# Four graph layers, stage of adj: layer 0's table rows stored from ACT's queue, and other ranks for the stage's pieces

## The chip, the cores and the metric

The kernel runs on one core of a Trainium2 chip. A core has five engines with a queue of instructions each: PE (matrix products), DVE (vector), ACT (scalar), POOL (general) and SP, which only starts transfers. Instructions of one queue go in order; queues wait for one another through semaphores. Transfers are moved by 16 DMA engines that all queues share. The metric is the device time of one execution in microseconds (us); lower is better.

## The reference, cut to what matters

3327 nodes with 512 float32 features each pass through four residual layers. All four use the same adjacency matrix, 3327 x 3327 int32, in which an entry is 1 with a probability of 0.0012, some four neighbours a node.

```python
def reference(x, adj, ...):
    # layer 0: mean over neighbours
    h = relu(layernorm(x))
    mask = adj > 0
    agg = mask @ h / max(deg, 1)
    x = x + relu(concat(h @ W_self + b_self, agg @ W_nb + b_nb) @ W_comb + b_comb)
    # layer 1: attention, 8 heads of 64; layer 2: 4 heads, quaternion weights, elu; layer 3: 1 head
    for attend in (layer1, layer2, layer3):
        h = relu(layernorm(x))
        Wh = h @ W                      # [n, heads, o]
        e = leaky_relu(src(Wh)[:, None] + dst(Wh)[None, :])
        x = x + act(softmax(where(adj > 0, e, -inf)) @ Wh)
    return x
```

No layer needs the dense product with adj: a node's sum runs over its few neighbours. The kernel finds them once and gathers rows. In layer 0 the two products behind each other are folded: `wf[1]` = W_nb · W_comb (lower half), `wf[0]` = W_self · W_comb (upper half), so a node needs z = h · `wf[1]` of its neighbours and y = h · `wf[0]` of itself.

## The kernel before, in words

The nodes lie in 26 tiles of 128 rows (the last has 127). A first stage, the stage of adj, does everything up to the first gather; then four layers run, in which POOL gathers rows of a table in device memory, PE sums them and makes the next table. Only the first stage is touched.

**Reading adj.** Each tile of adj is loaded in two halves of 128 x 1664 (`ai`, 832 KB, four buffers; line 1184, on SP). DVE finds the places of the ones in each half (line 1209, two instructions); ACT squares it with a running sum (line 1217, `junk`), which counts the ones for a check at the end. A buffer comes free when both have read it. From the places DVE makes lists of neighbours and degrees, and POOL writes them as a record beside the node's row (lines 1261 to 1267).

**Layer 0's rows.** Tiles go in pairs, in the order `SEQUENCE` (0 to 19, 25, 20 to 24). For each: x is loaded (SP, line 1184 too), DVE takes mean and variance (1309), ACT and DVE make the norm from it, ACT writes h (1328), PE transposes it into `pt` (1337), ACT copies that to `hT` (1342), and PE makes two products of four row blocks: z in `pz` and y in `py` (both line 1349). On the page a product of one tile counts as eight matmuls. ACT copies z to `zt` (two buffers; line 1358, or 1361 for the short tile) and the copy is stored, 256 KB, as the tile's rows of `table[0]` (line 1366). ACT copies y into the node's own row (1373).

**Weights.** Before any z, PE transposes W_nb and makes the four blocks of `wf[1]` (line 976; line 953 transposes), and the same with W_self for `wf[0]`; the blocks are copied by ACT and DVE in turn (line 989 ACT, 987 DVE). Later come the bias, the transposes of the last layer's weight W3 (PE 1094, copy on ACT 1100) and the products of weights with the attention vectors (POOL 1131), which DVE (1148), or ACT for the last layer (1142), sums.

**The sort.** When all tiles are searched, DVE makes a table of degree classes (1394), PE sums it (`pm_tot`, 1406), DVE works out each node's place (1419 to 1427), and POOL scatters the nodes' own rows (x, y and record) to their places in `own` (1435), one instruction per tile. SP reads the records back (1451), DVE makes degrees of them (1505, 1506), and the first gather of layer 0 starts (1562).

**What sets the order.** The instructions' order on each queue is worked out ahead of time by the class `Plan`. It keeps a list of pieces, each with an engine, an estimated cost, a rank, what it depends on, and the buffers that it takes and gives. It then plays the stage through: always the piece that can start earliest is taken, and among those that can start at the same time the one of lowest rank. Pieces on `"dma"` are transfers in this play and issue nothing. The helper `load` puts an issue on SP, cost 0.38, and a transfer behind it. The ranks come from eight numbers: `ORDER_W` gives those of the weights (1 and 0 for the two folded weights, the bias, and "later" for the other layers' weights); the adj tile at position k has `ADJ`·k; the pair that begins at position p0 has `WORK`·p0 + `WORK0`; its loads of x have `X0` + `X`·p0; y comes `SELF` later in rank than z. The sort has -1. The scatters, the read back and the degrees come behind the plan, in that order.

Of the kernel before, what the change touches and what calls it, by code (L numbers as in the profile page):

```python
# [8 lines left out]
F32 = mybir.dt.float32  # L9
# [9 lines left out]
P = 128  # L19
# [673 lines left out]
def gnn_stack_kernel(  # L693
# [19 lines left out]
    nc = tc.nc  # L713
    N, D = x_in.shape
# [20 lines left out]
    with ExitStack() as st:  # L735
# [82 lines left out]
        def rough(pool, tag, var, scale=1.0):  # L818

            n = var.shape[-1]  # L820
            ln = pool.tile([P, 2], F32, tag="ln", name=f"ln{tag}", bufs=3)[:, :n]
            nc.scalar.activation(ln, var, AF.Ln, bias=eps, scale=scale)
            r0 = pool.tile([P, 2], F32, tag="r0", name=f"r0{tag}", bufs=3)[:, :n]
            nc.scalar.activation(r0, ln, AF.Exp, bias=lift, scale=-0.5)
            return r0

        def refined(pool, tag, mv, r0):

            n = r0.shape[-1]
            a = pool.tile([P, 2], F32, tag="nra", name=f"nra{tag}", bufs=3)[:, :n]  # L830
            nc.vector.scalar_tensor_tensor(a, r0, -1.0, r0, ALU.mult, ALU.mult)
            nc.vector.scalar_tensor_tensor(a, mv[:, :, 1], EPS, a, ALU.add, ALU.mult)
            r = pool.tile([P, 2], F32, tag="rs", name=f"rs{tag}", bufs=3)[:, :n]
            nc.vector.scalar_tensor_tensor(r, a, 3.0 * LIFT * LIFT, r0, ALU.add, ALU.mult)
            nmr = pool.tile([P, 2], F32, tag="nmr", name=f"nmr{tag}", bufs=3)[:, :n]
            nc.vector.scalar_tensor_tensor(nmr, mv[:, :, 0], -1.0, r, ALU.mult, ALU.mult)
            return r, nmr

        def refined_sums(pool, tag, mv, r0):

            n = r0.shape[-1]
            a = pool.tile([P, 2], F32, tag="nra", name=f"nra{tag}", bufs=3)[:, :n]
            nc.vector.scalar_tensor_tensor(a, r0, -1.0 / D, r0, ALU.mult, ALU.mult)
            nc.vector.scalar_tensor_tensor(a, mv[:, :, 1], D * EPS, a, ALU.add, ALU.mult)
            r = pool.tile([P, 2], F32, tag="rs", name=f"rs{tag}", bufs=3)[:, :n]
            nc.vector.scalar_tensor_tensor(r, a, 3.0 * LIFT * LIFT, r0, ALU.add, ALU.mult)
            nmr = pool.tile([P, 2], F32, tag="nmr", name=f"nmr{tag}", bufs=3)[:, :n]
            nc.vector.tensor_tensor(nmr, mv[:, :, 0], r, ALU.mult)
            return r, nmr


        with tc.tile_pool(name="p0", bufs=1) as pa, tc.tile_pool(name="p0p", bufs=2, space=PSUM) as pp:
# [5 lines left out]
            later = pa.tile([P, NK - EARLY, ROW], F32, tag="later", name="later")  # L858
# [31 lines left out]
            bias = part("bias", D)  # L890
# [20 lines left out]
            plan = Plan(limits)  # L911
            tiles = {}
# [257 lines left out]
            o = put("pool", 3.0, (0.5, 0), empty_rows)  # L1170
# [125 lines left out]
            rows_in = []  # L1296
            for p0 in range(0, NK, 2):
                unit = SEQUENCE[p0 : p0 + 2]
                rank = (p0 * WORK + WORK0, 2)
                box = {}  # L1300
                seen = []
                for j, i in enumerate(unit):
                    o = load((X0 + p0 * X, j), 4.0 * P * D, start_x, (i,), free_at(i))

                    def stats(j=j, i=i, unit=unit, box=box):
                        if j == 0:
                            box["mv"] = new("mv", f"n{unit[0]}", [P, 2, 2])
                        st6 = pa.tile([P, 6], F32, tag="st6", name=f"st6n{i}", bufs=2)
                        nc.vector.bn_stats(st6, node(i)[:, :D])
                        nc.vector.bn_aggr(box["mv"][:, j, :], st6)  # L1310

                    seen.append(put("dve", 0.88, rank, stats, (), [o] + seen, take=("mv",) if j == 0 else ()))

                def guess(unit=unit, box=box):
                    box["r0"] = rough(pa, f"n{unit[0]}", box["mv"][:, :, 1])

                o = put("act", 0.6, rank, guess, (), seen)

                def refine(unit=unit, box=box):
                    box["r"], box["nmr"] = refined(pa, f"n{unit[0]}", box["mv"], box["r0"])  # L1320

                normed = put("dve", 0.8, rank, refine, (), [o], take=("norm",), give=("mv",))
                for j, i in enumerate(unit):
                    key = f"n{i}"

                    def relu(j=j, i=i, key=key, box=box):
                        h = new("h", key, [P, D])
                        nc.scalar.activation(
                            h, node(i)[:, :D], AF.Relu, bias=box["nmr"][:, j : j + 1], scale=box["r"][:, j : j + 1]
                        )  # L1330

                    o = put("act", 0.83, rank, relu, (), [normed], take=("h",), give=("norm",) if j == 1 else ())

                    def turn(key=key):
                        pt = new("pt", key, [P, DC, P], space=pp)
                        for c in range(DC):
                            nc.tensor.transpose(pt[:, c, :], tiles["h", key][:, c * P : (c + 1) * P], ident)

                    o = put("pe", 0.55, rank, turn, (), [o], take=("pt",), give=("h",))

                    def keep(key=key):
                        nc.scalar.copy(new("hT", key, [P, DC, P]), tiles["pt", key])  # L1342

                    o = put("act", 0.6, rank, keep, (), [o], take=("hT",), give=("pt",))

                    def multiply(s, tag, key=key):
                        pz = new(tag, key, [P, D], space=pp)
                        for c in range(DC):
                            nc.tensor.matmul(  # L1349
                                pz, tiles["hT", key][:, c, :], wf[s][:, c, :], start=(c == 0), stop=(c == DC - 1)  # L1350
                            )

                    z = put("pe", 3.5, rank, multiply, (1, "pz"), [o] + finished[1], take=("pz",))

                    def keep_z(i=i, key=key):
                        zt = new("zt", key, [P, D])
                        if i < NK - 1:
                            nc.scalar.copy(zt, tiles["pz", key])
                        else:

                            nc.scalar.activation(zt, tiles["pz", key], AF.Copy, scale=real[:, i : i + 1])

                    o2 = put("act", 0.62, rank, keep_z, (), [z], take=("zt",), give=("pz",))

                    def store(i=i, key=key):
                        nc.sync.dma_start(table[0][i * P : (i + 1) * P, :D], tiles["zt", key])
# [20 lines left out]
            o = put("dve", 0.3, sorting, work, (), [f for k in range(NK) for f in found_of[k]], take=("ai",))  # L1387
# [44 lines left out]
            landed = []  # L1432
# [83 lines left out]
        with tc.tile_pool(name="run", bufs=1, reuse_waits="tile") as pr, tc.tile_pool(  # L1516
# [9 lines left out]
            plan = Plan(limits)  # L1526
# [733 lines left out]
```

## Time and profile before

| what | value |
|---|---|
| median of three runs | 1074.55 us (1073.38 to 1076.67) |
| the profiled execution | 1231.77 us |
| its span in the records | 1230.0 us |
| granted PE clock, mean | 0.855 |
| first stage, to the first gather | 0 to 278.18 us |
| PE / DVE / ACT busy, whole span | 73% / 59% / 42% |

All positions below are us from the start of the span of the one profiled execution. That execution was 15% longer than the median of the runs without a profile, so differences are taken from its own times. A line of waits says which instruction waited, what it waited for, how long in total, how often, and the longest. A line of the timeline gives start and length of an instruction or a row of like ones, and in brackets the idle time of its engine ahead of it and what ended it. "SPq" is SP's queue, whose instructions only start transfers.

Two figures stand behind several of the prediction's steps. A product of one tile takes PE 3.44 us (24 matmuls in a row, three products, take 10.46 us at 214.65, the last one's end included). The 22 scatters from 219.24 to 246.36 follow each other at 1.26 us.

### The profile page before, as it was taken

The numbers are of one execution on the slowest core, as the hardware profiler recorded it, in microseconds if no ns is written. First come the engines' busy times: TensorE is split into PE (matmuls) and PEld (weight loads), VectorE is DVE, ScalarE is ACT, GpSimd is POOL, SyncE is SP. The second block draws the span as 40 slices with busy tenths as digits, with TensorE's granted clock in tenths as the row PEclk, the third lists the DMA queues.
The fourth block names the chain that finished last, engine by engine and source line by source line (L and its number), as shares of the span: only waits on it lengthen the run. The fifth ranks groups of instructions, "written<-read, shape, count | busy, mean of one in ns | idle before, by whom it ended". The sixth has DMA issues, their size and how long they took to land. (4 is left out here: it accounts for less than half of the span.)

```text
span 1230.0 us, 11605 instructions
## 1 busy us (share of the span) xinstructions
PE 901.8 (73%) x2853; PEld 510.4 (41%) x2853; DVE 726.6 (59%) x1848; ACT 518.2 (42%) x1700; POOL 610.1 (50%) x719
## 2 busy tenths in 40 slices
PE   7599999854098889752979796539979832948865
PEld 4244444322075656531647464214435421423322
DVE  6499989204176557453869784628894815534441
ACT  4488886210043433422656553316554621312221
POOL 1064246717655550175757511766883236675661
PEclk9899999977599899966989889659896956978987
DMA  9999894958587772265666521665754345575561
GB/s 352 338 364 338 294 306 146 317 203 286 172 268 252 247 249 89 76 195 149 198 183 178 154 79 55 189 187 150 209 169 129 91 121 149 168 206 160 163 186 59
DMA packets 89910, 240.49 MB, mean 196 GB/s; under 512 B 24933, under 2 KB 26477, under 8 KB 89834
## 3 DMA queue, kind: packets, MB, share of 16 engines
q0 software_dynamic: 41600, 137.72, 38.1%
q1 hardware_dynamic: 48234, 101.96, 23.3%
q8 instruction: 24, 0.39, 0.1%
q14 instruction: 52, 0.43, 0.1%
HBM read 190.35 MB, written 49.27 MB: 195 GB/s over the span
## 5 line engine op out<-in xcount | busy, mean ns | idle before, releaser
L1562 POOL DMA_INDIRECT ring<-table,nbr x351 | 368.5, 1050 | 185.5 <-issue 80.9
L1593 PE MATMUL acc<-ring,ident 128*128 128x512 f32 (+1 forms) x494 | 266.6, 676 | 66.8 <-DVE ring L2110 24.3
L1780 PE MATMUL pw<-w,hT 128*128 128x264 f32 (+1 forms) x832 | 197.3, 394 | 18.3 <-ACT hT L1705 13.6
L1780 PEld LDWEIGHTS pw<-w,hT 128*128 128x128 f32 x832 | 161.2, 195 | 60.9 <-ACT hT L1705 20.5
L1593 PEld LDWEIGHTS acc<-ring,ident 128*128 128x128 f32 (+1 forms) x494 | 98.7, 215 | 175.1 <-issue 107.5
L1562 POOL DMA_INDIRECT ring<-table,srec x117 | 110.1, 941 | 77.8 <-issue 31.5
L2110 DVE TENSOR_TENSOR ring<-ring,w 128x2048 f32<-128x2048 f32 (+7 forms) x76 | 114.3, 1531 | 4.7 <-DVE w L1978 3.0
L2060 PE MATMUL pw<-w,hT 128*128 128x512 f32 x208 | 101.7, 634 | 13.3 <-ACT hT L2052 11.0
L1209 DVE FIND_INDEX8 fidx<-one_i,ai 128x8 uint32<-128x832 int32 x104 | 104.2, 1018 | 0.0
L1349 PE MATMUL pz_n<-wf,hT_n 128*128 128x512 f32 x208 | 95.2, 609 | 10.9 <-ACT hT_n L1342 8.4
L1705 ACT ACTIVATE hT<-pt 128x128 f32<-128x128 f32 (+1 forms) x312 | 81.8, 292 | 39.7 <-PE pt L1694 18.5
L1217 ACT ACTIVATE junk<-ai 128x1664 int8<-128x1664 int32 (+1 forms) x52 | 82.7, 1590 | 32.6 <-DMA ai<-in_adj_dram 32.2
L1694 PE MATMUL pt<-ident,h 128*128 128x128 f32 x208 | 36.5, 312 | 75.9 <-ACT h L1676 73.4
L1349 PE MATMUL py_n<-wf,hT_n 128*128 128x512 f32 x208 | 91.9, 592 | 0.0
L1803 ACT COPY t<-pw 128x512 f32<-128x512 f32 (+1 forms) x54 | 30.6, 566 | 134.0 <-PE pw L1780 43.9
L1941 DVE TENSOR_TENSOR e<-ring,fs 128x24 f32<-128x24 f32 (+25 forms) x96 | 15.2, 172 | 120.2 <-DMA ring<-table,nbr 102.0
L2060 PEld LDWEIGHTS pw<-w,hT 128*128 128x128 f32 x208 | 42.3, 207 | 73.2 <-issue 51.3
L1705 ACT ACTIVATION_READ_ACCUMULATOR hT<-pt 128x1 f32 x312 | 69.5, 223 | 0.0
L1694 PEld LDWEIGHTS pt<-ident,h 128*128 128x128 f32 x208 | 28.1, 160 | 96.3 <-ACT h L1676 81.6
L2194 POOL MEMSET mark<- 1x1 f32 x3 | 0.3, 88 | 132.7 <-DMA table<-t 132.7
L1349 PEld LDWEIGHTS pz_n<-wf,hT_n 128*128 128x128 f32 x208 | 39.8, 195 | 62.8 <-issue 49.4
L2046 PE MATMUL pt<-ident,y 128*128 128x128 f32 x96 | 16.4, 312 | 67.4 <-issue 56.8
(185 smaller groups left out, 1319.7 us busy)
## 6 DMA issues: line engine op xcount, KB each, us to landing
ai<-in_adj_dram SPq DMA_DIRECT2D x25, 832.0 KB
ai<-in_adj_dram SPq DMA_DIRECT2D x25, 831.5 KB
table<-t SPq DMA_DIRECT2D x52, 258.0 KB
xy<-own SPq DMA_DIRECT2D x26, 512.0 KB
table<-t SPq DMA_DIRECT2D x26, 260.0 KB
table<-zt_n SPq DMA_DIRECT2D x26, 256.0 KB
ring<-table,nbr POOLq DMA_INDIRECT x351
later<-in_x_dram SPq DMA_DIRECT2D x15, 256.0 KB
```

Of the source, the lines that this page charges most:

```text
L1209: nc.vector.max_index(fidx[:, i, qq * 8 : (qq + 1) * 8], one_i, ai[:, q * QW : min(cols, (q + 1) * QW)])
L1217: nc.scalar.activation(junk[:, :cols], tiles["ai", key][:, :cols], AF.Square, accum_out=sq[:, i, hf : hf + 1])
L1349: nc.tensor.matmul(pz, tiles["hT", key][:, c, :], wf[s][:, c, :], start=(c == 0), stop=(c == DC - 1))
L1562: nc.gpsimd.indirect_dma_start(out=ring[:m, r0 + s, : width[layer]], out_offset=None, in_=table[layer], in_offset=bass.IndirectOffsetOnAxi ...
L1593: nc.tensor.matmul(acc, ident[:m, :], g[:m, s, :D], start=(k == 0), stop=(k == len(slots) - 1))
L1694: nc.tensor.transpose(pt[:, c, :], h[:, c * P : (c + 1) * P], ident)
L1705: nc.scalar.activation(hT[:, c, :n], pt[:, c, :n], AF.Copy, accum_out=hsum[layer][:, i, c : c + 1])
L1780: nc.tensor.matmul(pw[:, b, :w], tiles["hT", key][:, c, :], wsb[layer][:, c, b, :w], start=(c == 0), stop=(c == DC - 1),)
L1803: nc.scalar.copy(t[:, :D].rearrange("p (b f) -> p b f", b=2)[:, lo:hi, :], pw[:, lo:hi, :HD])
L2046: nc.tensor.transpose(pt[:, c, :], tiles["y", key][:, c * P : (c + 1) * P], ident)
L2060: nc.tensor.matmul(pw[:, 0, :], tiles["hT", key][:, c, :], w3[:, c, :], start=False, stop=(c == DC - 1))
L2110: nc.vector.tensor_tensor(v, v, box["w"][:m, j, lo:hi, :].unsqueeze(3).to_broadcast([m, hi - lo, H, O]), ALU.mult,)
```

## The change

There are three edits. The store of `zt` is started by ACT (`nc.scalar`) instead of SP, and in the plan it is a piece on ACT of cost 0.35 with a transfer behind it. The eight numbers behind the ranks get other values. The plan's transfer of a scatter costs 1.5 instead of 2.0. Besides, four small tiles of the norm become three columns wide, of which as many are used as before.

```diff
-ORDER_W = {1: -20.0, 0: -1.0, "bias": -4.0, "later": 20.0}
-ADJ, WORK, WORK0, X0, X, SELF = 1.0, 1.13, 1.2, -14.0, 1.77, 7.0
+ORDER_W = {1: -37.41, 0: -0.2, "bias": -17.46, "later": 14.56}
+ADJ, WORK, WORK0, X0, X, SELF = 1.0, 1.18, 0.3, -20.32, 2.18, 4.08
...
-            ln = pool.tile([P, 2], F32, tag="ln", name=f"ln{tag}", bufs=3)[:, :n]
+            ln = pool.tile([P, 3], F32, tag="ln", name=f"ln{tag}", bufs=3)[:, :n]
...
                     def store(i=i, key=key):
-                        nc.sync.dma_start(table[0][i * P : (i + 1) * P, :D], tiles["zt", key])
-
-                    rows_in.append(load(rank, 4.0 * P * D, store, (), [o2], give=("zt",)))
+                        nc.scalar.dma_start(table[0][i * P : (i + 1) * P, :D], tiles["zt", key])
+
+
+                    o2 = put("act", 0.35, rank, store, (), [o2])
+                    rows_in.append(plan.add("dma", 4.0 * P * D / 370e3, rank, None, [o2], lag=2.0, give=("zt",)))
...
-                landed.append(plan.add("dma", 2.0, (-1.0, pos), None, [o], lag=1.5))
+                landed.append(plan.add("dma", 1.5, (-1.0, pos), None, [o], lag=1.5))
```

What comes out as the order on each queue: the four blocks of `wf[0]` and the bias stand ahead of the first z on PE; the load of W3 (1 MB) stands ahead of adj tile 2 on SP; ACT's copy of the first `wf[0]` block stands ahead of its count of that tile instead of behind it, and DVE's copy of the second block behind that tile's finds. W3's transposes are spread between products, and the sums of line 1142 come earlier on ACT, as do POOL's products of line 1131. `pm_tot` stands on PE ahead of z of tile 20 instead of behind it. The loads of x of the last tiles stand ahead of the last adj loads on SP. The 26 stores follow their `zt` copies on ACT. Behind the stage the order on DVE's and SP's queues is the same as before.

More of the change, by code (lines that the diff above doesn't have):

```diff
@@ L820, in rough @@
             n = var.shape[-1]
-            ln = pool.tile([P, 2], F32, tag="ln", name=f"ln{tag}", bufs=3)[:, :n]
+            ln = pool.tile([P, 3], F32, tag="ln", name=f"ln{tag}", bufs=3)[:, :n]
             nc.scalar.activation(ln, var, AF.Ln, bias=eps, scale=scale)
-            r0 = pool.tile([P, 2], F32, tag="r0", name=f"r0{tag}", bufs=3)[:, :n]
+            r0 = pool.tile([P, 3], F32, tag="r0", name=f"r0{tag}", bufs=3)[:, :n]
             nc.scalar.activation(r0, ln, AF.Exp, bias=lift, scale=-0.5)
@@ L829, in refined @@
             n = r0.shape[-1]
-            a = pool.tile([P, 2], F32, tag="nra", name=f"nra{tag}", bufs=3)[:, :n]
+            a = pool.tile([P, 3], F32, tag="nra", name=f"nra{tag}", bufs=3)[:, :n]
             nc.vector.scalar_tensor_tensor(a, r0, -1.0, r0, ALU.mult, ALU.mult)
             nc.vector.scalar_tensor_tensor(a, mv[:, :, 1], EPS, a, ALU.add, ALU.mult)
-            r = pool.tile([P, 2], F32, tag="rs", name=f"rs{tag}", bufs=3)[:, :n]
+            r = pool.tile([P, 3], F32, tag="rs", name=f"rs{tag}", bufs=3)[:, :n]
             nc.vector.scalar_tensor_tensor(r, a, 3.0 * LIFT * LIFT, r0, ALU.add, ALU.mult)
-            nmr = pool.tile([P, 2], F32, tag="nmr", name=f"nmr{tag}", bufs=3)[:, :n]
+            nmr = pool.tile([P, 3], F32, tag="nmr", name=f"nmr{tag}", bufs=3)[:, :n]
             nc.vector.scalar_tensor_tensor(nmr, mv[:, :, 0], -1.0, r, ALU.mult, ALU.mult)
@@ L841, in refined_sums @@
             n = r0.shape[-1]
-            a = pool.tile([P, 2], F32, tag="nra", name=f"nra{tag}", bufs=3)[:, :n]
+            a = pool.tile([P, 3], F32, tag="nra", name=f"nra{tag}", bufs=3)[:, :n]
             nc.vector.scalar_tensor_tensor(a, r0, -1.0 / D, r0, ALU.mult, ALU.mult)
             nc.vector.scalar_tensor_tensor(a, mv[:, :, 1], D * EPS, a, ALU.add, ALU.mult)
-            r = pool.tile([P, 2], F32, tag="rs", name=f"rs{tag}", bufs=3)[:, :n]
+            r = pool.tile([P, 3], F32, tag="rs", name=f"rs{tag}", bufs=3)[:, :n]
             nc.vector.scalar_tensor_tensor(r, a, 3.0 * LIFT * LIFT, r0, ALU.add, ALU.mult)
-            nmr = pool.tile([P, 2], F32, tag="nmr", name=f"nmr{tag}", bufs=3)[:, :n]
+            nmr = pool.tile([P, 3], F32, tag="nmr", name=f"nmr{tag}", bufs=3)[:, :n]
             nc.vector.tensor_tensor(nmr, mv[:, :, 0], r, ALU.mult)
```

## The prediction

> **What bounds the kernel now.** The edits lie in the first stage: reading adj, sorting the nodes by degree, making layer 0's rows. I read first the busy time of each engine in stretches of it (columns: stretch, its length, busy us and instructions of PE, PEld, DVE, ACT and POOL, granted clock, DMA share, GB/s).
>
> ```profile
> 50.00:100.00 50.00, 47.15 (x126) 21.73 (x126) 47.35 (x120) 42.91 (x63) 19.33 (x35) 0.98 0.97 384
> 100.00:150.00 50.00, 50.00 (x142) 23.82 (x141) 47.10 (x145) 43.79 (x65) 16.49 (x56) 1.00 0.85 302
> 150.00:200.00 50.00, 47.62 (x139) 22.40 (x138) 43.18 (x118) 37.20 (x60) 25.90 (x48) 1.00 0.81 275
> 214.00:250.00 36.00, 26.83 (x74) 12.32 (x73) 9.22 (x32) 8.51 (x17) 25.43 (x39) 0.95 0.94 324
> ```
>
> From 50 to 200 us PE works 144.8 of 150 us, DVE 137.6, ACT 123.9: nothing has much slack, ACT most. After 214 everything has slack except the transfers. Next, what PE waits for up to 280 us (line waited for, total us, times, longest):
>
> ```profile
> PE pm_w L976 <- ACT wf L989: 10.3, 1, 10.3
> PE pz_n L1349 <- ACT hT_n L1342: 8.4, 2, 7.7
> PE pm_w L1094 <- ACT w L1100: 1.6, 1, 1.6
> PE pm_tot L1406 <- DVE ai_sort L1394: 1.3, 1, 1.3
> ```
>
> The 10.3 us lie at 38 to 49, the 7.7 at 244 to 251, so between 60 and 214 PE loses only about 3. Then SP's queue, up to 215 us:
>
> ```profile
> SPq L1184 <- DVE fidx L1209: 58.7, 29, 4.9
> SPq L1366 <- ACT zt_n L1358: 34.5, 12, 9.8
> SPq L1366 <- ACT zt_n L1361: 10.2, 1, 10.2
> ```
>
> Line 1366 is the store that moves. For 44.7 us SP stood before one of them until ACT had made its tile, with adj loads queued behind; the larger wait, 58.7, is DVE freeing adj buffers. Last, the timelines of PE and of ACT where the stage ends (start, length, instruction, idle before it):
>
> ```profile
> 214.30 0.34 PE L1406 MATMUL pm_tot<-ai_sort,ones 128*128 128x416 bf16 x1 [1.25 <-DVE ai_sort L1394]
> 251.33 6.20 PE L1349 MATMUL pz_n<-wf,hT_n 128*128 128x512 f32 x8 [7.70 <-ACT hT_n L1342]
> 257.38 10.46 PE L1349 MATMUL py_n<-wf,hT_n 128*128 128x512 f32 x24
> ```
> ```profile
> 239.29 0.58 ACT L1342 COPY hT_n<-pt_n 128x512 f32<-128x512 f32 x1 [5.08 <-issue]
> 250.69 0.58 ACT L1342 COPY hT_n<-pt_n 128x512 f32<-128x512 f32 x1 [10.82 <-remote]
> ```
>
> The sort starts at 214.30 with pm_tot; POOL's scatters of the nodes' own rows run from 219.24 without a break, the 22nd at 246.36, 1.26 us apart, and the DMA share is 0.94 meanwhile. ACT's two waits fall in that burst, have no producer named, and the second ends 3.4 us after the last scatter's issue finished (247.3). Then PE does four products (z of tile 24, y of 22, 23, 24) up to 267.84, the last scatter goes at 269.21, and 10.3 us after PE's end the first gather of layer 0 starts, at 278.18.
>
> **What the skill says.** The Trainium skill, "DMA: Bandwidth & Descriptors", section Issuing engines are not separate DMA queues: transfers run on the same 16 DMA engines whoever starts them, and only the sequencer's time is divided. So the moved store brings no bandwidth; it frees SP from its place in the queue. The trace of before can't test this, ACT starts no transfer in it. "Perfetto Trace Analysis", section DMA Instruction — HWDGE: the issuing sequencer is busy until the descriptors are handed over, and the movement is not in that time. The trace agrees: an issue of line 1366 takes 0.327 us (median of 26, longest 0.751) for 256 KB.
>
> **The change, part by part.**
>
> *Store on ACT.* 26 issues leave SP and enter ACT, each directly behind its zt copy. Price on ACT: 0.33 us, SP's row, plus the drain of the copy ahead; both bounds are open, since before has none. Low end 0.33, high end about 1.5 if the issue keeps ACT for the copy's drain and a slot in the queue; I take 0.55. ACT is idle 29.6 of the 154 us from 60 to 214 (124.42 busy), and 22 stores fall there: 12.1 us at 0.55. The cover is that idle time, 1.35 us a store; above it ACT becomes the bound. Queued behind a store on ACT are the next hT copy, h and the counting of adj, so PE would feel it first through hT. Nine of the 26 also wait for an older transfer's semaphore; those were mostly long done in before. I put the direct cost at 0.
>
> *SP without them.* 8.5 us of issues go (26 x 0.327) and the 44.7 us of waiting. But most adj loads were held by DVE's finds anyway, and DVE was short of adj data only 20.1 us from 46 to 219, of which 12.8 is one wait near 46. The other 7.3 can shrink; I take two thirds, 4.9 us. DVE's sort input, done at 214.25, comes at about 209.4. The x loads of the last tiles, at 212.93 in before behind a store that waited 10.2 us, now precede the last adj loads.
>
> *New order, start.* PE now makes all four wf0 blocks and the bias ahead of the first z; ACT's copy of block 0 stands ahead of the count of adj tile 2 instead of behind it, so the 10.3 us wait shrinks. But W3's 1 MB load now precedes adj tile 2 on SP (the trace lands 832 KB in 2.1 to 2.7 us: about 2.5 us later), and the copy of block 1 on DVE stands behind that tile's find. By hand: fourth block at 54.3 instead of 56.68, second z done at 64.8 instead of 64.0. Cost 0.8 us.
>
> *New order, middle.* W3's transposes and their copies are spread out: PE's waits of 1.6 at 156.45 and 0.7 at 161.23 go, gain 2.3. The attention sums on ACT (line 1142) move from 204 to 213 into 166 to 181, where h of tiles 18 and 19 would be ready at 186.9 and PE needs them at 187.7: 0.8 of slack.
>
> *New order, the sort.* pm_tot stands on PE before z of tile 20 instead of behind it: one product (3.44 us) moves behind the sort. PE could reach pm_tot at 214.30 - 1.25 + 0.8 - 2.3 - 3.44 = 208.1; DVE is ready at 209.4, which decides. So sort and scatters start 4.9 us earlier, scatters at about 214.3, burst over at 241.5. POOL's records (212.88 to 218.94 in before) must be earlier too; they can, since eight products of line 1131 that POOL did from 203 to 212.9 are done earlier.
>
> *The tail.* Behind pm_tot PE has 12 products and four sets of transposes, about 43 us (before 11, 39.6). If PE were held by its work alone, the end would move by 4.9 - 3.44 = 1.5 earlier. But in before it was held by ACT, until the burst ended; I take the hold to end with the burst. Then z of 24 starts at 246.4, and the same four products and 10.3 us follow. The small tiles' third column, and the scatter's price in the plan, issue nothing: 0. SP's read back of the sorted records is no longer queued behind two stores, but waited for the scatters anyway: 0.
>
> Sum: -4.9, all of it the burst; the early +0.8 and the middle -2.3 are hidden by DVE ahead of the sort. The profiled execution took 1231.77 us (span 1230.0), 15% over the median of 1074.55; the stage alone would have to be separated from that excess, which no view does, so I carry the difference unscaled: 1231.8 to 1226.9 profiled, 1074.55 - 4.9 = 1069.65, say 1069.7.
>
> **The rivals.** About 3.2 us (0.3%) is what a measurement tells from no change.
>
> *ACT becomes the bound* (slower). For: ACT is at 81% from 60 to 214, each store stands ahead of an hT copy, and tiles 18 and 19 have 0.8 us of slack. It decides above 1.35 us a store on average; at 1.55 it would cost 22 x 0.2 = 4.4 us, at 2 us 14.3. A local form: a block of sums at 166 to 181 delays hT by some 6 us which PE never gets back. Time 1078 to 1089, middle 1080. Against: SP's 0.33 us.
>
> *Hidden or given back* (same). DVE's work, not adj data, sets the sort: its idle time doesn't shrink, pm_tot stays near 213, the added product behind it eats the rest. For: DVE is busy 142.5 of 154 us. Time 1073 to 1076.
>
> *The whole tail wait goes* (larger gain). ACT's 5.08 and 10.82 us have no producer; if ACT, with its order changed, escapes them, PE's 2.2 and 7.7 us go, and the clock which made one product 6.20 instead of 3.6 recovers: 9.9 + 2.6, less part of the 3.44. With DVE's gain 1058 to 1063. Against: the cause, a full DMA, remains.
>
> *The store doesn't free SP*: adj loads wait for semaphores that ACT's stores now raise, so SP still stops behind them. It ends as the hidden case.
>
> **How the numbers follow.** Likeliest case 0.51 (1067 to 1072.5, of which 0.42 is faster by the bound and 0.09 same), the whole tail 0.11 (faster), hidden 0.10 (0.08 same, 0.02 slower), ACT bound 0.28 (0.27 slower, 0.01 same). Faster 0.53, same 0.18, slower 0.29. Range 1060 to 1081: it leaves out half of the whole-tail case and about a third of the ACT case, some 0.15 in all.
>
> **What would show it.** Right: the scatters start near 214 and pm_tot waits for DVE by a microsecond or two; SP has no wait of zt; PE's wait for wf is a few us; ACT's store issues are 0.3 to 0.6 us; the first gather starts near 273. Wrong: hT waits of PE between 60 and 210 (ACT bound); pm_tot near 213; ACT's nameless waits ending far from the last scatter, or none; loads of adj later than before at 46 by more than 3 us.

## The result: a third of a per cent slower

The changed kernel takes 1079.35 us (median of 18 runs) against 1075.47 for the kernel before, a ratio of 1.0038 with a 95% interval of 1.0021 to 1.0054. The forecast was 1069.7; the sign was wrong, and the measured time lies inside the range.

At some times every run, of whatever kernel here, takes about 1220 us instead of 1074, and the profiled execution that the prediction used was one of these. A second profile of the kernel before, of an execution of 1073 us, is therefore the one to compare with; it is called the second profile of before here. The two differ mainly behind the stage (952 us against 805 from the first gather to the end) and in the tail: ACT's two waits of 5.08 and 10.82 us, on which the forecast's tail was built, aren't in the second, and PE, which had slack behind the sort in the first, has none (35.71 of 36 us busy):

```profile
214.00:250.00 36.00, 35.71 (x96) 16.65 (x95) 7.92 (x29) 9.95 (x19) 26.08 (x36) 1.00 0.94 323
```

In the second profile of before PE waits for this, up to the last product of the stage:

```profile
PE pm_w L976 <- ACT wf L989: 10.7, 1, 10.7
PE pm_w L953 <- DMA later<-in_L_gnn_W_nb_dram: 6.4, 1, 6.4
PE pm_w L976 <- DVE wf L987: 2.7, 1, 2.7
```

In the changed kernel (lines from 1366 on are two higher, so pm_tot is line 1408):

```profile
PE pm_w L976 <- DVE wf L987: 17.4, 1, 17.4
PE pm_w L953 <- DMA later<-in_L_gnn_W_nb_dram: 6.4, 1, 6.4
PE pt_n L1337 <- ACT h_n L1328: 6.0, 1, 6.0
```

With the small ones, left out here, these are 22.2 and 31.0 us, 8.8 more. The last product of the stage ends at 253.5 in before and at 262.7 in the changed kernel, 9.2 later, with as many products in both. So the order of the work, not its amount, moved PE's end. The two places are seen on PE's timeline of the changed kernel:

```profile
56.15 5.97 PE L976 MATMUL pm_w<-later 128*128 128x512 f32 x8 [17.38 <-DVE wf L987]
...
183.61 1.11 PE L1337 MATMUL pt_n<-ident,h_n 128*128 128x128 f32 x4 [5.97 <-ACT h_n L1328]
184.52 4.86 PE L1349 MATMUL py_n<-wf,hT_n 128*128 128x512 f32 x8
...
219.22 0.34 PE L1408 MATMUL pm_tot<-ai_sort,ones 128*128 128x416 bf16 x1
```

and the same place in the second profile of before:

```profile
212.88 0.34 PE L1406 MATMUL pm_tot<-ai_sort,ones 128*128 128x416 bf16 x1 [0.80 <-DVE ai_sort L1394]
```

Both stalls cost more than their length. The Trainium skill, "TensorE: Matmul & The Clock Gate", section Part 1: The HAM clock gate, says that PE falls to half its clock after an idle window of a few microseconds and needs as long to come back. The trace agrees in kind: the granted clock is 0.50 from 56 to 60 and from 184 to 186, and 1.00 from 62 and from 188 on; the eight matmuls behind the 17.38 us gap take 5.97 us, those behind the 5.97 us gap 4.86, others 3.60. Before pays some of this too: its block behind the 10.7 us gap takes 5.32.

The sort comes 6.3 us late (219.22 against 212.88), the first scatter 5.8 (223.66 against 217.83), the first gather of layer 0 6.3 (272.75 against 266.49). From there to the end the two profiles take 803.7 and 804.5 us, so the loss lies in the stage. Its size is better taken from the medians: they differ by 3.9 us, not 6.3, and a profile is one execution. The windows of before, then of the changed kernel (columns as in the prediction), show where engines fell idle:

```profile
50.00:100.00 50.00, 47.34 (x127) 21.98 (x126) 46.05 (x117) 41.54 (x60) 19.34 (x35) 0.98 0.97 379
...
150.00:200.00 50.00, 48.81 (x142) 22.95 (x141) 44.05 (x121) 37.28 (x61) 25.66 (x48) 1.00 0.80 276
```
```profile
50.00:100.00 50.00, 43.85 (x114) 20.50 (x115) 46.52 (x118) 40.77 (x58) 26.16 (x67) 0.89 0.94 362
...
150.00:200.00 50.00, 44.03 (x118) 20.51 (x116) 41.69 (x122) 33.27 (x61) 27.11 (x48) 0.93 0.73 244
```

From 50 to 100 PE loses 3.5 us of work, from 150 to 200 4.8; in the second stretch DVE (2.4), ACT (4.0) and the transfers lose too. All of them wait for each other there.

PE isn't the only engine that comes late to the sort. DVE's table of degree classes is ready at 217.8 against 212.8, 5.0 later, and PE adds 1.5 behind it. Of DVE's waits from 40 to 218, first in before, then in the changed kernel, the one for adj is as long as it was; those for POOL's products and for the norm's first part on ACT have grown:

```profile
DVE fidx L1209 <- DMA ai<-in_adj_dram: 19.1, 5, 13.3
...
DVE nran L831 <- ACT r0n L824: 1.2, 1, 1.2
```
```profile
DVE fidx L1209 <- DMA ai<-in_adj_dram: 18.9, 5, 16.6
DVE w L1148 <- POOL later L1131: 5.1, 2, 2.8
DVE nran L831 <- ACT r0n L824: 5.0, 2, 4.3
```

The longest of each of these two, 2.8 and 4.3 us, end at 168 and 178.5, in the same stretch as PE's second stall.

How that stall comes about can be followed in the changed kernel. POOL's records of tiles 12 to 17 wait for DVE's lists, and stand ahead of the clearing of tile 25's two adj buffers (line 1200):

```profile
158.16 0.63 POOL L1261 TENSOR_SCALAR none<-nid,null_f 128x96 f32<-128x96 f32 x1 [2.97 <-DVE nid L1255]
...
163.86 2.91 POOL L1200 MEMSET ai<- 128x1664 int32 x2
```

In before that clearing stands at 145.9 and 148.6. SP issues nothing from 156.7 until the first of the two is cleared, and the adj loads behind it wait as well:

```profile
155.86 0.81 SPq L1184 DMA_DIRECT2D later<-in_x_dram  x2
165.37 0.33 SPq L1186 DMA_DIRECT2D ai<-in_adj_dram  x1
```

ACT then stands before the count of an adj tile that isn't there, and 2.6 us more before the next, with the norm and h of later tiles queued behind; DVE and PE follow:

```profile
171.07 1.59 ACT L1217 ACTIVATE junk<-ai 128x1664 int8<-128x1664 int32 x1 [6.05 <-DMA ai<-in_adj_dram]
```

### The profile page after: what moved, and what is told of

It reads as the page before. It is cut to its first block, busy times and chain, and to the rows that moved or that the text cites. A ratio compares the mean times of both kernels' runs of the same rounds, so it can differ in the third digit from the quotient of the medians.

```text
span 1076.4 us, 11583 instructions
## 1 busy us (share of the span) xinstructions
PE 868.5 (81%) x2853; PEld 494.1 (46%) x2853; DVE 723.0 (67%) x1848; ACT 519.5 (48%) x1700; POOL 622.1 (58%) x719
## 5 line engine op out<-in xcount | busy, mean ns | idle before, releaser
L1564 POOL DMA_INDIRECT ring<-table,nbr x351 | 379.5, 1081 | 115.3 <-issue 59.5
L1595 PE MATMUL acc<-ring,ident 128*128 128x512 f32 (+1 forms) x494 | 255.5, 651 | 74.9 <-DVE ring L2112 47.8
L1782 PE MATMUL pw<-w,hT 128*128 128x264 f32 (+1 forms) x832 | 192.4, 388 | 3.2 <-ACT hT L1707 3.2
L1782 PEld LDWEIGHTS pw<-w,hT 128*128 128x128 f32 x832 | 158.7, 192 | 42.8 <-ACT hT L1707 10.1
L1595 PEld LDWEIGHTS acc<-ring,ident 128*128 128x128 f32 (+1 forms) x494 | 94.3, 206 | 178.9 <-issue 77.1
L1943 DVE TENSOR_TENSOR e<-ring,fs 128x24 f32<-128x24 f32 (+25 forms) x96 | 15.3, 171 | 136.3 <-DMA ring<-table,nbr 128.5
L2062 PE MATMUL pw<-w,hT 128*128 128x512 f32 x208 | 97.7, 614 | 5.1 <-ACT hT L2054 5.1
L1349 PE MATMUL pz_n<-wf,hT_n 128*128 128x512 f32 x208 | 92.0, 593 | 0.0
L1707 ACT ACTIVATE hT<-pt 128x128 f32<-128x128 f32 (+1 forms) x312 | 81.6, 291 | 15.8 <-PE pt L1696 15.3
L2062 PEld LDWEIGHTS pw<-w,hT 128*128 128x128 f32 x208 | 40.6, 198 | 60.7 <-issue 46.3
L1970 ACT ACTIVATE ex<-el 128x48 f32<-128x48 f32 (+19 forms) x56 | 12.8, 233 | 110.2 <-DVE el L1953 110.2
L822 ACT ACTIVATE ln<-mv,eps 128x1 f32<-128x1 f32 (+1 forms) x60 | 18.0, 300 | 98.0 <-DVE mv L1652 88.6
L2048 PE MATMUL pt<-ident,y 128*128 128x128 f32 x96 | 15.6, 294 | 57.1 <-DVE y L2032 50.7
L2098 ACT ACTIVATE ring<-ring,w 128x64 f32<-128x64 f32 (+1 forms) x216 | 57.8, 361 | 4.2 <-DVE w L1980 3.1
```

Of the source, the lines that this page charges most:

```text
L1349: nc.tensor.matmul(pz, tiles["hT", key][:, c, :], wf[s][:, c, :], start=(c == 0), stop=(c == DC - 1))
L1564: nc.gpsimd.indirect_dma_start(out=ring[:m, r0 + s, : width[layer]], out_offset=None, in_=table[layer], in_offset=bass.IndirectOffsetOnAxi ...
L1595: nc.tensor.matmul(acc, ident[:m, :], g[:m, s, :D], start=(k == 0), stop=(k == len(slots) - 1))
L1707: nc.scalar.activation(hT[:, c, :n], pt[:, c, :n], AF.Copy, accum_out=hsum[layer][:, i, c : c + 1])
L1782: nc.tensor.matmul(pw[:, b, :w], tiles["hT", key][:, c, :], wsb[layer][:, c, b, :w], start=(c == 0), stop=(c == DC - 1),)
L2048: nc.tensor.transpose(pt[:, c, :], tiles["y", key][:, c * P : (c + 1) * P], ident)
```

## The experiments

No kernel here leaves any work out. The profile positions named are those of one execution each. Where the same kernel was profiled twice, its sort lay 4.0 us apart in one case (215.7 and 219.7) and 1.2 to 1.4 in three (212.6 and 211.4, 214.3 and 212.9, 218.4 and 217.0), so differences below some 4 us are no evidence by themselves.

Where only the place of a piece changes, the plan is played as before and pieces are then moved in the list that it gives, so that everything else keeps its place:

```diff
+    def moved(self, seq):
+        for what, where in self.MOVES if any("name" in o for o in seq) else ():
+            op = next(o for o in seq if o.get("name") == what); seq.remove(op); k = next(k for k, o in enumerate(seq) if o.get("name") == where.lstrip("+")); seq.insert(k + where.startswith("+"), op)
+        return seq
...
-        for _, _, op in sorted(order, key=lambda o: o[:2]):
+        for op in self.moved([o[2] for o in sorted(order, key=lambda o: o[:2])]):
```

A move names a piece and the piece ahead of which it goes, or behind which, with a "+". `pm02` is PE's block 2 of wf[0] and `wf02` its copy; `load2_0`, `find2_0` and `square2_0` are load, DVE's search and ACT's count of the first half of the third adj tile (positions count from 0 in `SEQUENCE`, so tile 25 has position 20); `rec12` is POOL's records of tiles 12 to 17; `m230` is a product of layer 2's weights; `raw3`, `raw2`, `ab1` and `w10` to `w17` are loads of weights and attention vectors. Line numbers stay those of the kernel that is edited.

### Is it the store or the order?

The kernel before once more, unchanged:

> The kernel before, profiled once more. If the profiled execution of before was not typical, its 10.8 us wait of ACT ahead of an hT copy at 240 to 251 and PE's 7.7 us behind it are gone here, the stage's last product ends near 255 instead of 267.8, and the first gather starts near 266. If the waits belong to the kernel (a transfer engine full of scatters), they stand at the same place with 8 us or more.

ACT's wait and PE's 7.7 us were gone; the last product ended at 253.5, the first gather came at 266.49. The nameless waits aren't in this execution.

The changed kernel with the store back on SP, everything else in place:

```diff
-                        nc.scalar.dma_start(table[0][i * P : (i + 1) * P, :D], tiles["zt", key])
+                        nc.sync.dma_start(table[0][i * P : (i + 1) * P, :D], tiles["zt", key])
```

> The changed kernel, its 26 stores issued by SP again; every other instruction stands where it stood. Theory order (PE lost its time to two stalls, 17.4 us for a wf block near 38 to 56 and 6.0 us for h near 178, both made by the new order): both stalls stay, time 1078 to 1081. Theory store (0.40 us of ACT's time for each store is what slowed it): time 1074 to 1076.

Measured: 1081.2, ratio 1.0067 (1.0042 to 1.0092). Both stalls stay:

```profile
PE pm_w L976 <- DVE wf L987: 14.8, 1, 14.8
...
PE pt_n L1337 <- ACT h_n L1328: 6.3, 2, 5.1
```

The other half, the kernel before with the store on ACT in the old order:

```diff
-                        nc.sync.dma_start(table[0][i * P : (i + 1) * P, :D], tiles["zt", key])
+                        nc.scalar.dma_start(table[0][i * P : (i + 1) * P, :D], tiles["zt", key])
```

> The kernel before, its 26 stores issued by ACT, all else in the old order. Theory order: no loss, 1072 to 1076. Theory store: 1079 or more, with waits of PE for hT between 60 and 210.

Measured: 1075.37, ratio 1.0011 (0.9992 to 1.0030). With the store on SP in both, the new order costs 0.67%, clear of noise: the order makes the loss. With the new order the store on ACT may even be worth something (1.0038 against 1.0067), but the intervals overlap.

How far the store's engine costs nothing needs care, because this kernel doesn't place its stores as the changed one does. In its plan the store is still a piece of SP, and in 19 of 26 cases it falls behind ACT's next instruction instead of directly behind the `zt` copy. The issue then lies within that instruction and ACT loses no time:

```profile
105.66 1.60 ACT L1217 ACTIVATE junk<-ai 128x1663 int8<-128x1663 int32 x1
105.80 0.33 ACTq L1366 DMA_DIRECT2D table<-zt_n  x1
```

In the changed kernel 25 of 26 stand directly behind the copy, and ACT waits for its end first:

```profile
177.49 0.33 ACTq L1366 DMA_DIRECT2D table<-zt_n  x1
177.86 0.30 ACT L822 ACTIVATE lnn<-mv_n,eps 128x2 f32<-128x2 f32 x1 [0.40 <-ACT zt_n L1358]
```

Moving the changed kernel's stores to SP takes this away and brings 38.0 us of SP's waits for `zt` back, so the two runs don't show that ACT's price adds nothing to the loss. They show that the new order loses without it.

### Which stall?

The late wf copies: blocks and copies of wf[0] moved ahead of adj tile 2, for which they had waited.

```diff
+    MOVES = (("pm02", "find2_0"), ("wf01", "find2_0"), ("pm03", "find2_0"), ("wf02", "find2_0"), ("wf03", "find2_0"),)
```

> The changed kernel with four pieces moved: the copies of wf[0]'s blocks 1, 2 and 3, and PE's blocks 2 and 3, ahead of the reading of adj tile 2 by DVE and ACT, so that they don't stand behind a transfer that lands at 51. Theory order: PE's 17.4 us wait falls below 5, the first z starts near 43 instead of 62.2, and the time falls by 4 to 9, to 1070 to 1075. Rival (DVE's searches set the sort, PE would wait there instead): the sort stays at 217 to 219 and the time at 1077 to 1079.

Measured: 1078.39, ratio 1.0044 (1.0025 to 1.0062). The first z starts at 42.43 instead of 62.2, and nothing comes of it: PE's waits only change their names.

```profile
PE pt_n L1337 <- ACT h_n L1328: 12.5, 2, 7.5
PE pz_n L1349 <- ACT hT_n L1342: 7.5, 1, 7.5
```

PE's lead of 20 us is gone by the sort (218.34 against 219.22). What it waits for comes from ACT, and ACT's h and hT stand behind the counts of adj tiles. The rival's outcome, so, and its reason holds in part: DVE is ready at 215.9, still 3.1 later than in before, and PE, held by ACT, adds 2.4.

The records, moved behind the clearing, alone and with the early copies:

```diff
+    MOVES = (("rec12", "+load20_1"),)
```

> The changed kernel with one piece moved on POOL: the records of tiles 12 to 17 stand behind the clearing of the two adj buffers of tile 25 (line 1200) instead of ahead of it. Theory jam (the clearing at 163.9, 17 us later than in before, holds all adj loads behind it on SP, then ACT, then PE): clearing near 155, the last adj load from 205.7 to 198 or earlier, PE's 6.0 us wait for h below 2, the sort from 219.2 to 212 to 215, time 1072 to 1075. Rival (the early stall for the wf blocks is what counts): the sort moves by less than 2, time 1077 to 1080.

> The changed kernel with both: the wf copies and blocks ahead of adj tile 2, and the records of tiles 12 to 17 behind the clearing of tile 25's buffers. Theory jam: the early lead of PE, worth nothing alone (1078.4), now counts, because nothing holds ACT and DVE at 165 to 180: below the kernel with the records moved alone by 2 to 5, 1067 to 1072. Rival (DVE's own work sets the sort): the same time as with the records moved alone.

The records alone: clearing at 159.8 and 161.7, far from the 155 expected, sort at 218.40, 1219.01 us against 1219.44 for before (six runs, no interval). With both: sort at 215.71, ratio 1.0041 (0.9978 to 1.0104). The clearing didn't come earlier because it then waited for the buffers themselves, which DVE frees. They were run again:

> Once more the changed kernel with the records of tiles 12 to 17 behind the clearing of tile 25's buffers, because its first run was taken while the kernel before took 1219 us. Its sort stood at 218.4 there, 0.8 earlier than in the changed kernel: if positions carry over, ratio 1.002 to 1.005, no clear gain.

> Once more both moves, the early wf copies and the records. Sort near 215.7 as in its first run. Theory two stalls: between the changed kernel (1.0038) and the one with the products moved too (1.0027), 1.002 to 1.004; if the products' place counts for nothing, the same as with them, 1.0027.

Ratios 1.0012 (0.9980 to 1.0045) and 0.9934 (0.9875 to 0.9994), sorts at 217.0 and 219.7. The second contradicts its own first run, and also the medians of all its runs (1224.43 against 1220.88); nothing can be built on either.

W3's load, moved behind adj tile 2 and half of tile 3:

```diff
+    MOVES = (("raw3", "+load3_0"),)
```

> The changed kernel with W3's 1 MB load moved on SP behind the loads of adj tile 2 and of the first half of tile 3. Theory jam: adj tile 2 lands 2 to 4 us earlier, PE's 17.4 us wait shrinks by as much, but the jam at 165 to 180 takes it back: 1077 to 1080. Rival (the late start is what counts): the sort comes 2 to 4 us earlier and the time falls to 1074 to 1077.

Ratio 1.0055 (1.0002 to 1.0109). DVE's first search of tile 2 starts at 48.1 instead of 50.8 and PE's wait is 13.6 instead of 17.4, as expected; the sort comes at 217.9. No gain to be seen, in an interval too wide to exclude a small one.

All three moves together, the third being POOL's last two products of layer 2, for which DVE waited in the kernel with two moves (one wait of 6.6 us):

```diff
+    MOVES = (("m230", "rec12"), ("m231", "rec12"), ("rec12", "+load20_1"), ("pm02", "find2_0"), ("wf01", "find2_0"), ("pm03", "find2_0"), ("wf02", "find2_0"), ("wf03", "find2_0"),)
```

> The changed kernel with three moves at once: the wf[0] copies and blocks ahead of adj tile 2; on POOL the last two products of layer 2's weights ahead of the clearing of tile 25's buffers, and the records of tiles 12 to 17 behind it. Theory two stalls (the late wf copies, and POOL's order around the clearing, which makes DVE wait 5 to 8 us for a product): DVE's wait for products below 1.5, the sort at 208 to 212, first gather within 2 of the 266.5 of before, ratio 0.997 to 1.001. Rival (DVE's sums standing ahead of searches are the loss, whatever POOL does): sort at 214 or later, ratio 1.002 or more.

Measured: 1075.71 against 1073.19, ratio 1.0027 (1.0013 to 1.0041). DVE's wait for products fell from 5.1 to 1.7 us, its sort input was ready at 214.0 instead of 217.8, the first gather came at 269.98 instead of 272.75. That is 2.8 of the 6.3 us in the stage, less than two profiles of one kernel have differed by; in the whole time the gain over the changed kernel isn't beyond the intervals. Of the two theories the rival's numbers were met (sort at 216.4, ratio 1.0027); its reason, DVE's sums ahead of the searches, has the next kernel against it, where these sums lie at 162 to 205 us instead of 127 to 171 and the sort comes at 217.2. That the two stalls are part of the loss is likely, and not shown.

### Which numbers?

Only the rank of the later layers' weights put back, which takes POOL's products and DVE's sums away from the clearing:

```diff
-ORDER_W = {1: -37.41, 0: -0.2, "bias": -17.46, "later": 14.56}
+ORDER_W = {1: -37.41, 0: -0.2, "bias": -17.46, "later": 20.0}
```

> The changed kernel with one number of before: the rank of the later layers' weights 20.0 instead of 14.56. The start of the stage stays as in the changed kernel; POOL's products of weights with attention vectors (14 of them ahead of the clearing of tile 25's adj buffers in the changed kernel, 2 around it in before) and DVE's sums of them go back behind the searches. Theory later (those products and sums hold adj's reading): the first clearing near 146 to 150 instead of 163.9, DVE's wait for POOL's products gone, the sort near 212 to 215, the ratio to before within 0.2% of 1. Rival start (the 17.4 us stall counts): ratio 1.003 to 1.005, as the changed kernel.

Measured: 1087.81, ratio 1.0130 (1.0093 to 1.0167). The clearing moved to 148.7, DVE's wait for products went, its sort input came at 217.1: as expected up to there, except that this is hardly earlier than 217.8. Here PE was early and waited 2.9 us for DVE, so DVE's lateness alone is enough for a late sort. But now SP's queue had loads of attention vectors ahead of x of the last tiles, and these wait for POOL's products:

```profile
SPq L1116 <- POOL later L1131: 17.4, 2, 15.3
SPq L1184 <- POOL later L1131: 12.6, 1, 12.6
```

So z of the last two tiles came behind the check's flag on PE, and the last product ended at 271.0. The theory that this one rank made the loss fell.

The other six numbers put back, the weights' ranks as changed:

```diff
-ADJ, WORK, WORK0, X0, X, SELF = 1.0, 1.18, 0.3, -20.32, 2.18, 4.08
+ADJ, WORK, WORK0, X0, X, SELF = 1.0, 1.13, 1.2, -14.0, 1.77, 7.0
```

> The changed kernel with the other six numbers of before (adj 1.0, pairs 1.13 and 1.2, x -14.0 and 1.77, y 7.0), the weights' ranks as changed. Theory later: the jam stays (14 products and the records ahead of the first clearing), sort at 217 or later, ratio 1.003 to 1.008. Rival (the pairs' ranks made the loss): ratio 0.998 to 1.002.

Measured: 1086.22, ratio 1.0121 (1.0087 to 1.0156); DVE was ready for the sort at 213.2, PE came to it only at 218.29, and the last product ended at 269.1. And all four weights' ranks put back, the six as changed:

> The changed kernel with all four ranks of the weights of before (-20, -1, -4, 20) and the other six numbers as changed: the fourth corner beside before's order, the changed one, and the one with old pair ranks. If each half of the numbers has an effect of its own, 1.0038 / 1.0121 predicts 0.992 to 0.995. If the numbers only fit together as a set, 1.005 or more, with the last tiles' loads of x or products late at the end.

Measured: 1081.02, ratio 1.0079 (1.0051 to 1.0106). The search of tile 2 started at 48.3 there, 2.5 us earlier than in the changed kernel, and the sort still came at 216.6 and the last product at 264.9. Two halves that cost 1.2% and 0.8% make 0.4% together: the numbers have no effects of their own that could be added. They choose one interleaving each. No run has all eight old numbers with the changed plan's other two edits, the store as a piece of ACT and the cheaper scatter; what these alone do to the order is open.

### What sets the end of the stage?

The kernel before with the wf copies early, twice:

```diff
+    MOVES = (("pm01", "square2_0"), ("wf00", "square2_0"), ("pm02", "square2_0"), ("wf01", "square2_0"), ("pm03", "square2_0"), ("wf02", "square2_0"), ("wf03", "square2_0"),)
```

> The kernel before with the copies of all wf[0] blocks, and PE's blocks 1 to 3, ahead of the reading of adj tile 2. PE's 10.7 and 2.7 us waits go. If PE sets the end of the stage here, the time falls by 3 to 8, to 1067 to 1072; if DVE's searches set the sort (pm_tot waited 0.8 us for them), by less than 2.

> Once more the kernel before with all wf[0] copies, and PE's blocks 1 to 3, ahead of the reading of adj tile 2. If DVE's searches set the sort, ratio 0.998 to 1.001; if PE sets the end of the stage, 0.993 to 0.997.

Ratios 0.9934 (0.9882 to 0.9986) and then, with 22 runs, 1.0012 (0.9995 to 1.0030). The intervals don't meet; the second, narrower one is taken, as the medians of the first run (1222.11 against 1219.44) show no gain either. PE's 13.4 us of waits for wf are gone, and it waits 6.7 for h and 2.7 for hT instead; the sort comes at 211.38, 1.5 earlier.

The kernel before with weights that are needed late moved behind adj tiles 10 to 12 on SP:

```diff
+    MOVES = (("raw3", "+load12_1"), ("ab1", "+load11_1"), ("raw2", "+load11_1"), ("w17", "+load10_1"), ("w16", "+load10_1"), ("w15", "+load10_1"), ("w14", "+load10_1"), ("w13", "+load10_1"), ("w12", "+load10_1"), ("w11", "+load10_1"), ("w10", "+load10_1"),)
```

> The kernel before with weights that are needed only after 100 us (layer 1's, layer 2's, W3, the first attention vectors; 2.8 MB) loaded behind adj tiles 10 to 12 on SP instead of ahead of tile 2. Adj tile 2 lands near 32 instead of 47, DVE's 13.3 us wait falls below 4. If DVE's searches set the sort, it moves from 212.2 to 203 to 208 and the ratio is 0.991 to 0.997; if PE's order does, the ratio is 0.998 to 1.002.

Measured: 1069.91 against 1073.19, ratio 0.9971 (0.9956 to 0.9985). DVE starts tile 2 at 39.3 instead of 46.7, its longest wait is 5.7 instead of 13.3 us (more of it comes back later, 15.3 in all against 19.1), and PE's wait for a wf copy shrinks from 10.7 to 2.6.

The sort comes at 210.23, the first gather at 263.31, 3.2 earlier than in before; the median is 3.3 us lower. That is less than was expected on both counts, but this version beats both kernels. With the early copies on top:

> The same, and the wf[0] copies and blocks 1 to 3 ahead of the reading of adj tile 2. DVE and PE both start earlier: ratio 0.988 to 0.995 if these two set the stage's end; 0.998 to 1.002 if the scatters' transfers or ACT do.

Measured: 1077.75, ratio 1.0038 (1.0020 to 1.0056). Now the copies stand ahead of the searches while PE hasn't made the blocks yet, and DVE waits for PE:

```profile
DVE wf L987 <- PE pm_w L976: 11.0, 2, 6.2
```

Tile 2 starts at 46.6 again, the sort at 218.9. Moving a copy ahead cost more here than it gave, because useful work stood behind it.

The positions in the kernels that were measured against 1073 to 1076 us of before (us; "DVE ready" is the end of its table of classes, the last column the time from the first gather to the end):

| kernel | ratio to before | DVE ready | pm_tot | first scatter | last product ends | first gather | rest |
|---|---|---|---|---|---|---|---|
| before | 1 | 212.8 | 212.9 | 217.8 | 253.5 | 266.5 | 804.5 |
| store on ACT alone | 1.0011 | 215.0 | 215.2 | 221.1 | 255.8 | 268.7 | 801.8 |
| changed | 1.0038 | 217.8 | 219.2 | 223.7 | 262.7 | 272.8 | 803.7 |
| changed, store on SP | 1.0067 | 217.6 | 219.1 | 223.5 | 262.5 | 274.2 | 805.1 |
| changed, early copies | 1.0044 | 215.9 | 218.3 | 222.8 | 261.8 | 272.5 | 807.9 |
| changed, three moves | 1.0027 | 214.0 | 216.4 | 220.8 | 259.8 | 270.0 | 810.7 |
| changed, old later rank | 1.0130 | 217.1 | 217.2 | 223.3 | 271.0 | 281.0 | 807.5 |
| changed, six old ranks | 1.0121 | 213.2 | 218.3 | 222.7 | 269.1 | 279.0 | 807.8 |
| changed, four old weight ranks | 1.0079 | 216.0 | 216.6 | 221.3 | 264.9 | 275.1 | 803.3 |
| before, early copies | 1.0012 | 211.3 | 211.4 | 216.3 | 252.0 | 264.7 | 803.3 |
| before, weights later | 0.9971 | 210.2 | 210.2 | 215.2 | 250.8 | 263.3 | 803.0 |
| before, weights later, early copies | 1.0038 | 218.9 | 218.9 | 223.9 | 259.5 | 271.9 | 805.6 |
| changed, old later rank, early copies | 1.0102 | 215.9 | 215.9 | 221.5 | 269.6 | 279.5 | 801.1 |

Two lines read from it. Where the last product is early, the first gather comes 47.5 to 48.7 us behind the first scatter (the five kernels built on before). Where it is late, the gather comes 9.9 to 10.2 us behind the last product (the four with some of the ranks put back). In the changed kernel and with three moves both hold nearly at once (49.1 and 49.2 us; 10.1 both); early copies (49.7 and 10.7) and the store on SP (50.7 and 11.7) fit neither well. The last column varies by 9.6 us although nothing behind the stage was changed, so the time of one profiled execution says little; the ratios do.

The table's last kernel, the old later rank with the early copies:

> The changed kernel with the later rank of before and with the wf[0] copies and PE's blocks 2 and 3 ahead of adj tile 2. Theory later: with the jam gone PE's early lead can last; 1 to 6 us below the kernel with the later rank alone, ratio to before 0.994 to 0.999. If DVE's searches set the sort, the same as with the later rank alone.

Measured: 1084.75, ratio 1.0102 (1.0067 to 1.0138), sort at 215.93, last product at 269.6: the tail of the last tiles' x, as with the later rank alone.

## Why the prediction was wrong

**What bounds the kernel.** Right in that PE, DVE and ACT are all nearly full from 50 to 214, and that the sort and the transfers set the end. Wrong in that everything but the transfers has slack after 214: PE is full there in the second profile. That reading came from a profile that wasn't typical, and the waits in it that had no producer should have warned.

**The store on ACT.** The price was right: the issue takes 0.327 us and ACT's work resumes 0.40 after the end of its copy, where without a store it starts 0.10 before that end. That is 0.50; I took 0.55. The Trainium skill's statement ("DMA: Bandwidth & Descriptors", Issuing engines are not separate DMA queues) agrees with the runs: with the store alone moved nothing is gained, the ratio is 1.0011. The rival that ACT becomes the bound through the stores, above 1.35 us each, is excluded by that price.

**SP without them.** This is the first step that failed, and the forecast's 4.9 us rested on it alone. I let two thirds of DVE's remaining wait for adj go because SP no longer stood before a store. None of it went: DVE's wait for adj is 18.9 us in the changed kernel and 20.4 with the store alone moved, against 19.1 in before, and its sort input comes at 217.8 and 215.0 against 212.8. SP's 42.0 us of waits for `zt` went, and its waits for adj buffers that DVE frees grew from 67.4 to 88.8 with the store alone moved, and to 92.1 in the changed kernel. The adj loads were held by the freeing of buffers, as the larger wait of SP (58.7 us) said.

**New order, start.** I wrote 0.8 us; it is 5.0 (the transposes of tiles 2 and 3 start at 69.17 against 64.18). Adj tile 2 is searched at 50.8, 4.1 later where I took 2.5, and the last block then runs at the lower clock, 5.97 us for 3.60. But the size wasn't what mattered: with the whole stall taken out the sort came 0.9 earlier, within what two profiles of one kernel differ by.

**New order, middle.** I wrote a gain of 2.3 from waits that went. They did go, but only 0.5 of W3's wait is in the second profile of before, and a wait of 6.0 with a slow product came. The 0.8 us of slack for tiles 18 and 19 was named, and the local rival put some 6 us there; the place and size were right. The reason wasn't: not the sums on ACT alone, but a count of adj on ACT whose tile was held by POOL's clearing. That the rival's 1078 to 1089 holds the measured time is luck to that extent. That POOL's queue is part of the path of adj's reading, and that DVE would wait 5.1 us for its products and 3.8 more for ACT's part of the norm, I had not priced at all.

**New order, the sort.** I expected DVE to decide at 209.4. DVE was ready at 217.8, and PE, 1.5 later still, decided at 219.2. Moving one product behind the sort made PE's end a limit besides: from `pm_tot` to the last product's end it takes 43.5 us, in before 40.6.

**Hidden by DVE.** The sum let early losses of PE vanish behind DVE. In part that is so: taking the 17.4 us stall away alone gave nothing that could be measured. But losses in a stage where four queues wait for each other can't be cleared against the one that seems latest.

What stays open: the two stalls are seen in the trace, and taking both away, with the products' place, brings back 2.8 of 6.3 us in one profile and no gain in time beyond the intervals. What the rest is, whether other pieces of the order, ACT's half microsecond a store or the price of the moves themselves, wasn't settled. That the new order slows the kernel, without the store on ACT too, is shown.

## What to carry to other kernels

Where an order is found for estimated durations, look first at transfers that land later than the plan thinks: in the plan's own play DVE begins adj tile 2 at 33 us, on the chip at 47 to 51, and everything placed behind it on DVE and ACT stood still. Loads that are needed late were better placed behind the first ones that are needed now, even where their queue would be idle; that alone gave 0.3%. And a wait that is removed counts only when what replaces it has been followed on each queue: of a lead of 20 us on PE (first z at 42.4 instead of 62.2) 5 were left at the second pair of tiles (68.3 instead of 73.5).

## What the runs showed of the hardware

An issue on ACT takes what one on SP takes, 0.327 us (median of 26 each). What it costs ACT depends on its place. Directly behind the copy that it stores, the next compute instruction starts 0.40 to 0.42 us after the copy's end (23 of 26 in the changed kernel), where without a store it starts some 0.10 before it (18 copies in the second profile of before). With one instruction between copy and issue, the next starts 0.07 to 0.11 before the end of that instruction, as if there were no issue (14 of the 19 such stores of the kernel with the store alone moved; at the other five ACT waits for something else or is idle). A kernel with all its stores one instruction later in the new order was not run.

And with 26 scatters, issued in about 37 us, 47.5 to 48.7 us pass from the first issue to the first gather, whenever the work that feeds the last of them is early enough. That their transfers set this is likely, not tested: SP's read back, which waits for them, starts 6.7 us after the last scatter in the second profile of before, and 3.8 in the changed kernel, whose last scatters come further apart.
